# The second layer's front on the spectrum by image pairs, with repeated rows in one transfer

## The chip, the cores and the metric

The kernel runs on one core of one Trainium2 chip. The core has TensorE (PE in the profile, its weight loads PEld), VectorE (DVE), ScalarE (ACT), GpSimd (POOL) and SyncE (SP, which issues most transfers; ACT issues some too), 16 DMA engines, SBUF as working memory and PSUM[...]. The metric is device time in microseconds (us) of one execution; the median over the runs counts, and lower is better.

## The reference

The input x is four images of 48x48 positions and 128 channels. Two layers are applied, each as x + layer(gn(x)), where gn normalises over groups of four channels. Layer 0 is a selective scan: an input projection, a 3x3 depthwise convolution, and for each of four scan directions a linear recurrence over 2304 positions with 16 states for 256 channels, then a normalisation, a gate and an output projection. Layer 1 reads the same array differently. It takes each image as 48 "time" planes of 48x128 pixels and does a spectral attention over them:

```
xa   = x.reshape(B * T, 1, H, W)                # 192 planes of 48 x 128
xa_n = inorm(xa)                                # per plane: mean 0, variance 1
k, q = fno(xa_n, wK), fno(xa_n, wQ)             # 32 heads, at half the resolution
v    = fno(xa_n, wV)                            # 32 heads, at full resolution
attn = softmax(q k^T / sqrt(d))                 # 48 x 48 for each image and head
att  = inorm(fno(attn v, wP) + xa)
m    = fno(fno(inorm(att), wM0), wM1)           # two more spectral layers, gelu between
out  = inorm(m) + att
```

fno is a spectral convolution (a 2-D Fourier transform, a complex weight on the low frequencies, the inverse transform) plus a pointwise product. All data are float32.

## The kernel before

`layer0` (from L54) works image by image and, for each, through four directions of five chunks of 480 positions (the last of them 384). A chunk has 16 steps, one per state. A step is spread over the engines: ACT computes the decay (`da`), DVE multiplies `db` (three steps in four; POOL the fourth) and runs the scan `h`, POOL multiplies `hc`, and PE sums `yp`. SP fetches the rows `cbc` and `bbc` for a step five steps before they are read out. `advance` writes this order out by hand: `on` keeps the order of the program on each engine. After every step `advance` calls `piece`, which runs one piece of a generator in the list `later`: the projections of the next direction, the `front` of the next image (group statistics, projection in, convolution), or `back`, which finishes a chunk and stores it to `x1_dram`. While the last image (image 3) is worked on there is no next front, so `later` holds projections and backs only. The buffer rings of layer 0 nearly fill SBUF.

`layer1` uses `nc` for most of its first half. Such instructions are put into each engine's order by a planner, which goes by the program's order, its own costs and what each instruction depends on; it may draw them forward into idle time of layer 0's end. The front of layer 1 does, in this order of the program: load constants and `xa` (L745, all four images, 192 planes at once); `gw`, the products of wP and wV, transposed and stored as `dgt` with each row written 16 times (L779 to L794); `spectral_weights` (L950), which makes the 96x96 matrices of the last two spectral layers and stores them as `sp_d`; group statistics by `gblk` copies and bn_stats (L993, L994), and the affine pass over `xa` (L1000); `first_norm` (L695), with mean and variance of each plane by products with `mean_m` (L700, L711); `prepare`, which loads wQ and wK in small pieces (L894 to L900) and multiplies them to `g_qk`; `forward_w` (L724), the transform along W by products with `fw` (L730), scaled by the plane's 1/deviation and written to DRAM; `load_a2`, which reads it back with h on the partitions (L741); transposes of `xa` into `pair_t` (L1024); and the selection of frequencies for q and k and the plain part (L1042 to L1073).

Then come the scores (L1109 to L1138, with `keys` beside them storing `dxt`), the softmax, and the readout (L1196 to L1274). The readout goes over two image pairs and four groups of eight frequencies. A group has three tiles `xrep` of 16 time rows each, with every row on eight partitions: two images by eight copies of 16 rows, 16 transfers of 72 KB a tile from SP (L1228). It has four tiles `grep` (L1236). For each tile and each of the four `grep`, DVE and POOL multiply to `v` and `v3`, and PE sums `acc` (L1253). `xrep`, `v` and `v3` have two buffers, `grep` four. The weights `wpv` and `mask` are loaded just ahead (L1196, L1197). The last part, from `p0` on, is two strands of 96 planes through the inverse transforms and the two spectral layers.

Of the kernel before, what the change touches and what calls it, by code (L numbers as in the profile page):

```python
# [53 lines left out]
def layer0(ctx, tc, io, x1_dram):  # L54
# [8 lines left out]
    const = ctx.enter_context(tc.tile_pool(name="l0_const", bufs=1))  # L63
    one = ctx.enter_context(tc.tile_pool(name="l0_one", bufs=1))
# [4 lines left out]
    small = ctx.enter_context(tc.tile_pool(name="l0_small", bufs=2))  # L69
    ps_s = ctx.enter_context(tc.tile_pool(name="l0_pss", bufs=1, space=PSUM))  # L70
    ps_b = ctx.enter_context(tc.tile_pool(name="l0_psb", bufs=1, space=PSUM))
    ps_a = ctx.enter_context(tc.tile_pool(name="l0_psa", bufs=1, space=PSUM))
# [185 lines left out]
    def front(b, made):  # L258
# [20 lines left out]
        yield  # L279

# [306 lines left out]
    for j, chunks in enumerate(directions):  # L587
# [9 lines left out]
        for m, c in enumerate(chunks):  # L597
            c.carry = carries[j % 2]
            for i in range(N):
                if k == ORDER[0] and b + 1 < B and m > 1 and coming is None and not any(g in later for g in backs):  # L600
                    coming = front(b + 1, images[b + 1])
                    later.append(coming)
                if i in (N // 2 + 3, N // 2 + 6):
                    f = int(i > N // 2 + 3)
                    if m + 1 < len(chunks):
                        while not (j or chunks[m + 1].ready):
                            piece()
                        drive(chunks[m + 1], f)
                    elif nxt is not None:
                        drain(nxt)  # L610
                        drive(directions[j + 1][0], f)
                advance(Step(c, i))
                if not chunks[-1].ready and not j:
                    piece()
    for _ in range(len(window)):
        advance(None)
    while later:
        piece()

# [24 lines left out]
def layer1(ctx, tc, io, x1_dram, out):  # L644
# [5 lines left out]
    nc = tc.nc  # L650
    img = ctx.enter_context(tc.tile_pool(name="l1_img", bufs=1))
    const = ctx.enter_context(tc.tile_pool(name="l1_const", bufs=1))
    small = ctx.enter_context(tc.tile_pool(name="l1_small", bufs=2))
    dram = ctx.enter_context(tc.tile_pool(name="l1_dram", bufs=1, space=DRAM))
# [9 lines left out]

    ident = load("ident1", [128, 128], io["c_ident"])
    gmat = load("gmat1", [128, 128], io["c_group"])
    fw = load("fw", [128, 66], io["c_FW"])
    fh = load("fh", [96, 96], io["c_FH"])
    fhi = load("fhi", [96, 96], io["c_FHI"])
    ih = load("ih", [96, 96], io["c_IH"])  # L670
    eps = const.tile([128, 1], F32, name="eps1")
    nc.gpsimd.memset(eps, 1e-5)
    mean_m = const.tile([128, 128], F32, name="mean_m")
    nc.gpsimd.memset(mean_m, 1.0 / (H * W))
    n_g = everywhere("n_g", io["L1_norm_g"], 6)
# [3 lines left out]

    turn = [0]  # L680

    def either():
        turn[0] += 1
        return nc.gpsimd if turn[0] % 3 == 0 else nc.vector
# [8 lines left out]
    def per_image(t, n=HB):  # L693
        return t[:, None, :].to_broadcast([128, n, BT])

    def first_norm(psum, work, x):

        pm = psum.tile([128, 512], F32, tag="st", name="pm_in")
        for q in range(H // 2):
            nc.tensor.matmul(pm[:, 0 : 2 * BT], mean_m, x[:, 2 * q : 2 * q + 2], start=(q == 0), stop=(q == H // 2 - 1))  # L700
        m = small.tile([128, BT], F32, tag="in_m", name="in_m")
        nc.scalar.copy(m, pm[:, 0:BT])
        nc.vector.tensor_add(m, m, pm[:, BT : 2 * BT])
        pv = psum.tile([128, 512], F32, tag="st", name="pv_in")
        for q in range(0, H, HB):
            d = x[:, q : q + HB]
            either().tensor_sub(d, d, per_image(m))
            sq = work.tile([128, HB, BT], F32, tag="blk", name=f"sq_{q}")
            nc.scalar.activation(sq, d, AF.Square)
            for j in range(0, HB, 2):  # L710
                nc.tensor.matmul(  # L711
                    pv[:, 0 : 2 * BT], mean_m, sq[:, j : j + 2], start=(q + j == 0), stop=(q + j == H - 2)
                )
        r = small.tile([128, BT], F32, tag="in_r", name="in_r")
        nc.scalar.copy(r, pv[:, 0:BT])
        nc.vector.tensor_add(r, r, pv[:, BT : 2 * BT])
        nc.scalar.activation(r, r, AF.Sqrt, bias=eps)
        nc.vector.reciprocal(r, r)
        nc.vector.tensor_scalar(r, r, n_g[:, 0:1], None, ALU.mult)
        return r  # L720

    def forward_w(psum, work, src, r, name):


        da = dram.tile([2, 33, H, BT], F32, name=f"da_{name}")
        for q in range(0, H, HB):
            a = work.tile([66, HB, BT], F32, tag="blk", name=f"a_{name}{q}")
            for j in range(0, HB, 2):
                p = psum.tile([128, 512], F32, tag="mm", name=f"pa_{name}{q}_{j}")
                nc.tensor.matmul(p[0:66, 0 : 2 * BT], fw, src[:, q + j : q + j + 2], start=True, stop=True)  # L730
                nc.vector.tensor_mul(
                    a[:, j : j + 2], p[0:66, 0 : 2 * BT].rearrange("p (a t) -> p a t", t=BT), per_image(r, 2)[0:66]
                )
            nc.sync.dma_start(da.rearrange("c k h t -> (c k) h t")[:, q : q + HB], a)
        return da

    def load_a2(a2, da, n):
        for c in range(2):
            for i, s in enumerate(range(0, n, 11)):
                e = min(s + 11, n)  # L740
                dmas[i % 2].dma_start(a2[c * 48 : (c + 1) * 48, s:e], da[c, s:e].rearrange("k h t -> h k t"))  # L741

    xa = img.tile([128, H, BT], F32, name="xa")
    for b in range(B):
        dmas[b % 2].dma_start(xa[:, :, b * T : (b + 1) * T], x1_dram[b])  # L745

    pair_t = [img.tile([128, H, 128], F32, tag=f"p{p}", name=f"xnt{p}") for p in range(2)]
    sp_d = [dram.tile([96, 32, 96], F32, name=f"sp_d{i}") for i in range(2)]
# [4 lines left out]
    dgt = dram.tile([4, NH, 16, 3 * NC], F32, name="dgt")  # L753
    with ExitStack() as pw:
        ps_t = pw.enter_context(tc.tile_pool(name="l1_wt", bufs=2, space=PSUM))
        q1 = pw.enter_context(tc.tile_pool(name="l1_w1", bufs=1))

        w_p = q1.tile([128, 12, 2, NH], F32, name="w_p")
        w_v = q1.tile([128, 6, 2, NH], F32, name="w_v")
        d48 = [q1.tile([128, 128], F32, name=f"d48{c}") for c in range(2)]  # L760
        for c in range(2):
            dmas[c].dma_start(w_p[:, :, c], io["wP"][c].rearrange("(j p) h -> p j h", p=128))
            dmas[c].dma_start(w_v[:, :, c], io["wV"][c].rearrange("(j p) h -> p j h", p=128))
            dmas[c].dma_start(d48[c], io[("c_D48r", "c_D48i")[c]])
        for c in range(2):
            p = ps_t.tile([128, 512], F32, tag="tr", name=f"pv48{c}")
            nc.tensor.matmul(p[:, 0:NH], d48[c], w_v[:, 0, c], start=True, stop=True)
            nc.scalar.copy(w_v[:, 0, c], p[:, 0:NH])
        gw = q1.tile([128, 12, 3, NH], F32, name="gw")
        for c in range(2):  # L770
            nc.vector.tensor_mul(gw[:, :, c], w_p[:, :, c], ws_v[:, None, :].to_broadcast([128, 12, NH]))
        half = [128, 6, NH]
        for c in range(2):
            g6 = gw[:, 0:6, c]
            t1 = q1.tile(half, F32, tag="gt", name=f"gt{c}_0")
            nc.vector.tensor_mul(t1, w_v[:, :, c], ws_p[:, None, :].to_broadcast(half))
            nc.vector.tensor_add(g6, g6, t1)
            for i in range(2):

                t2 = q1.tile(half, F32, tag="gt", name=f"gt{c}_{i + 1}")  # L780
                nc.vector.tensor_mul(t2, w_p[:, 0:6, i], w_v[:, :, (c + i) % 2])
                (nc.vector.tensor_sub if c == 0 and i == 1 else nc.vector.tensor_add)(g6, g6, t2)
        nc.vector.tensor_add(gw[:, :, 2], gw[:, :, 0], gw[:, :, 1])

        for k in range(4):
            gt = q1.tile([NH, 3, NC], F32, name=f"gtt{k}")
            for c in range(3):
                p = ps_t.tile([128, 512], F32, tag="tr", name=f"pgt{k}_{c}")
                for j in range(3):
                    nc.tensor.transpose(p[0:NH, j * 128 : (j + 1) * 128], gw[:, 3 * k + j, c], ident)  # L790
                nc.scalar.copy(gt[:, c], p[0:NH, 0:NC])
            nc.sync.dma_start(
                dgt[k], gt.rearrange("h c n -> h (c n)")[:, None].to_broadcast([NH, 16, 3 * NC])
            )  # L794
# [29 lines left out]
    def prepare():  # L824
# [30 lines left out]

        cqk = pe.tile([T, NH], F32, name="cqk")
        nc.vector.tensor_mul(cqk, ws_q[0:T], ws_k[0:T])
        nc.vector.tensor_mul(
            d_qk, ident[0:T, None, 0:T].to_broadcast([T, NH, T]), cqk[:, :, None].to_broadcast([T, NH, T])
        )  # L860
        with ExitStack() as pw:
# [21 lines left out]
            def weights(side, name, ws, gen, zero, mirror):  # L883
# [949 lines left out]
```

## Time and profile before

| what | us |
|---|---|
| median of 3 runs | 5072.27 (5071.78 to 5079.84) |
| the profiled execution | 5081.34 |
| its span, first to last instruction | 5079.4 |
| layer 0, to the issue of the last x1 store | to 4200.6 |
| front of layer 1, to the first product f of the scores | 4200.6 to 4407.4 |
| scores and softmax | 4407.4 to 4515.5 |
| wpv, mask and a0 | 4515.5 to 4543.8 |
| readout | 4543.8 to 4812.6 |
| inverse transforms, spectral layers, output | from 4814.3 |
| busy in the whole span | PE 4207.3, DVE 4169.1, POOL 4034.6, ACT 2923.0 |
| mean granted TensorE clock | 0.929 |

The chain of waits follows the work that ended last back from the end, at each step to what released it; what stands in it sets the time. Busy time by stretch tells whether an engine fills a stretch. A wait names the engine and line that waited, what ended the wait, the total in us, how often, and the longest.

### The profile page before, as it was taken

Reading aid. Unit: us, or ns where it says so; the run is one execution under the profiler, and the core shown is the slowest. Engines: PE = TensorE matmul, PEld = TensorE weight load, DVE = VectorE, ACT = ScalarE, POOL = GpSimd, SP = SyncE. Lnnn points to the kernel's source line nnn. Section 1 sums busy time; section 2 is a strip of 40 time slices with the busy share of each in tenths; the row PEclk is TensorE's granted clock in tenths of the full one; section 3 lists DMA queues with packets and bytes.
Section 4 is the critical chain, followed back from the end, with each engine's and each line's share of the span. In section 5 each row is a group of like instructions: output and inputs, shape, how many; then the busy total and the mean of one; then the engine's idle time right before and its main releaser. Section 6 shows DMA issues by size and latency. Waiting matters only on the chain. (4 is left out here: it accounts for less than half of the span.)

```text
span 5079.4 us, 44364 instructions
## 1 busy us (share of the span) xinstructions
PE 4207.3 (83%) x12344; PEld 1893.5 (37%) x12344; DVE 4169.1 (82%) x2888; ACT 2923.0 (58%) x6467; POOL 4034.6 (79%) x2219
## 2 busy tenths in 40 slices
PE   6889898888798988887989888878787785888876
PEld 2334333333343333333433333333333332453343
DVE  3689998989899989898999898999999873356636
ACT  3566566666565666665656666656666652223334
POOL 4589998988899989888999898999999873246532
PEclk9989999999899999998999999999999987889977
DMA  1223232322233323222333232333332216236646
GB/s 54 73 88 101 92 114 92 101 88 98 94 106 105 106 91 101 88 98 94 106 103 107 91 102 88 97 105 106 100 103 92 97 66 131 59 82 171 162 106 153
DMA packets 276766, 509.25 MB, mean 100 GB/s; under 512 B 100602, under 2 KB 185434, under 8 KB 276326
## 3 DMA queue, kind: packets, MB, share of 16 engines
q1 hardware_dynamic: 265318, 502.61, 32.5%
q10 hardware_dynamic: 11200, 3.81, 0.5%
q8 instruction: 97, 1.59, 0.1%
q14 instruction: 151, 1.24, 0.1%
HBM read 462.58 MB, written 43.72 MB: 100 GB/s over the span
## 5 line engine op out<-in xcount | busy, mean ns | idle before, releaser
L50 POOL TENSOR_TENSOR hc<-h,cbc 128x960 f32<-128x960 f32 (+1 forms) x1280 | 2719.7, 2140 | 449.2 <-DVE h L50 338.4
L50 DVE TENSOR_TENSOR_SCAN h<-da,carry,db 128x961 f32<-128x961 f32 (+1 forms) x1280 | 2702.4, 2129 | 153.8 <-ACT carry L50 106.0
L50 ACT ACTIVATE da<-dt,a_neg 128x480 f32<-128x480 f32 (+1 forms) x2560 | 1661.3, 649 | 1233.9 <-DVE h L50 1189.3
L50 PE MATMUL yp<-hc,ident 128*128 128x480 f32 (+1 forms) x5120 | 2273.9, 572 | 6.6 <-POOL hc L50 6.4
L50 PEld LDWEIGHTS yp<-hc,ident 128*128 128x128 f32 x5120 | 1006.3, 198 | 1409.7 <-issue 1018.9
L50 DVE TENSOR_TENSOR db<-du,pb 128x960 f32<-128x960 f32 (+1 forms) x960 | 1063.8, 1108 | 232.2 <-PE pb L50 176.8
L50 POOL TENSOR_TENSOR db<-du,bbc 128x960 f32<-128x960 f32 (+1 forms) x320 | 688.6, 2152 | 0.0
L50 PE MATMUL pb<-bs,pick 112*128 112x480 bf16 (+1 forms) x960 | 359.2, 374 | 391.3 <-DVE db L50 389.9
L50 PE MATMUL pc<-pad,cdiag 128*128 128x480 f32 (+1 forms) x630 | 284.6, 564 | 9.0 <-ACT pad L50 9.0
L1249 POOL TENSOR_TENSOR v<-grep,xrep 128x768 f32<-128x768 f32 x96 | 174.1, 1820 | 115.9 <-PE acc L1253 57.7
L1253 PE MATMUL acc<-v,attn_c 128*64 128x384 f32 x1152 | 214.8, 514 | 28.0 <-POOL v L1249 17.8
L1245 DVE TENSOR_TENSOR v<-gp,xrep 128x1536 f32<-128x1536 f32 x96 | 165.1, 1754 | 86.8 <-DMA xrep<-dxt 35.2
L50 POOL TENSOR_TENSOR du<-dt,xc 128x480 f32<-128x480 f32 (+1 forms) x160 | 205.0, 1282 | 37.2 <-ACT dt L50 37.2
L50 ACT COPY db<-carry 128x1 f32<-128x1 f32 x1280 | 226.7, 177 | 7.5 <-DVE db L50 4.2
L50 PE MATMUL px<-xc,w_xp 128*112 128x480 f32 (+1 forms) x320 | 215.0, 759 | 17.0 <-ACT xc L50 13.3
L50 PEld LDWEIGHTS <-pick 112*128 112x128 bf16 x960 | 97.9, 102 | 335.4 <-issue 311.8
L50 ACT ACT_TABLE_LOAD x147 | 188.6, 1283 | 25.7 <-PE gv_g L50 13.8
L50 PE MATMUL pd<-xd,w_dt 8*128 8x480 f32 (+1 forms) x320 | 167.6, 604 | 39.3 <-ACT bs L50 24.4
L50 ACT COPY carry<-h 128x2 f32<-128x2 f32 x1024 | 193.2, 189 | 0.0
L50 PEld LDWEIGHTS pc<-pad,cdiag 128*128 128x128 f32 x630 | 122.1, 195 | 142.4 <-issue 114.7
L50 PE MATMUL yp<-y,ident 128*128 128x480 f32 (+1 forms) x240 | 164.6, 815 | 0.2
L1253 PEld LDWEIGHTS acc<-v,attn_c 128*64 128x64 f32 x1152 | 89.8, 142 | 149.2 <-issue 65.8
(366 smaller groups left out, 3128.9 us busy)
## 6 DMA issues: line engine op xcount, KB each, us to landing
cbc<-cd SPq DMA_DIRECT2D x512, 480.0 KB
bbc<-cd SPq DMA_DIRECT2D x256, 240.0 KB
cbc<-cd SPq DMA_DIRECT2D x128, 384.0 KB
xrep<-dxt SPq DMA_DIRECT2D x384, 72.0 KB
grep<-dgt SPq DMA_DIRECT2D x32, 576.0 KB
bbc<-cd SPq DMA_DIRECT2D x64, 192.0 KB
dgt<-gtt SPq DMA_DIRECT2D x4, 2304.0 KB
x<-in_xT SPq DMA_DIRECT2D x16, 288.0 KB
```

Of the source, the lines that this page charges most:

```text
L50: return lambda *args, **kw: self._tc.keep_in_program_order(emit(*args, **kw))
L1245: nc.vector.tensor_mul(v, gp[:, None, :, 0:NC].to_broadcast([128, 2, 2, NC]), x[:, :, 0:2])
L1249: nc.gpsimd.tensor_mul(v3, r[:, 2:3].to_broadcast([128, 2, NC]), x[:, :, 2])
L1253: nc.tensor.matmul(acc[c][64 * b : 64 * b + 64, 0:NC], attn_c[:, 2 * pair + b, g, q], v[:, b, c] if c < 2 else v3[:, b], start=first, stop ...
```

## The change

Layer 1's program now opens by running layer 0 inside itself (`first_layer`), so that its own tiles can be laid on the right-hand side of SBUF.

- The input images go to `x_in`, two tiles of an image pair each, on the right-hand side. Images 0 to 2 are loaded whole, image 3 by the chunks in which layer 0 stores it.
- The front is done by pairs p = 0 and 1. `statistics` runs bn_stats straight on `x_in`. The affine pass is dropped: its scale goes into the transform's weights (`fwa`), its shift into a bias (`fwb`). The plane's mean is taken off the lowest frequency of the transform, averaged over h (`over_h`), and its 1/deviation `r` is multiplied onto `a2` after the reload instead of before the store. `first_norm` gets means and variances by products with 32 columns to four partition quarters, and writes x - mean to `xa`. Pair 0 is left to the planner (`by = nc`), pair 1 is in program order (`by = on`).
- `spectral_weights` becomes `matrices`, a generator in `later` of layer 0 while image 3 is worked on. The same generator arranges wQ and wK in DRAM (`d_w`, `d_m`); `products` (the second half of `prepare`) loads them with two transfers a side.
- `gw` comes after the pairs in the program, and `dgt` holds each row once.
- `xrep` is loaded by two transfers a tile with a leading repeat of 8, `grep` with each row repeated 16 times in the transfer, `wpv` and `mask` by 8 and 3 transfers.
- `ih` is loaded ahead of the last part. Pools change their order (`ps_a` first in PSUM, `small` earlier).

```diff
+    def matrices():
+        room = one.tile([128, 9, 128], F32, tag="cdiag", name="matrices")
...
+        general = [(0, 0, 8), (8, 12, 12), (20, 8, 4)]
+        for of, name in enumerate(("wQ", "wK")):
+            at_8 = 24 + 4 * of
+            for c in range(2):
...
+                for o, r, m in general + [(at_8, 8, 4)]:
+                    for j in range(4):
+                        k = int(j == 0)
+                        nc.sync.dma_start(dst[j][k:, o : o + m], src[j][k:, r : r + m])
+                    yield FREE
...
+        for n in range(2):
+            for k in range(0, 32, 2):
+                for c in range(2):
+                    for i in range(2):
+                        on.scalar.activation(m[3 + 2 * c + i], m[2], AF.Copy, scale=w[:, n, c, k + i : k + i + 1])
+                    if c == 0:
+                        yield FREE
+                p = side(f"psp{n}_{k}")
+                for c in range(2):
+                    on.tensor.matmul(
+                        p[0:96, 0:192],
+                        m[c],
+                        room[:, (3 + 2 * c) * 96 : (5 + 2 * c) * 96],
+                        start=(c == 0),
+                        stop=(c == 1),
+                    )
+                yield
+                on.scalar.copy(room[:, 7 * 96 : 9 * 96], p[0:96, 0:192])
+                nc.sync.dma_start(
+                    sp_dram[n][:, k : k + 2].rearrange("p k m -> p (k m)"), room[:, 7 * 96 : 9 * 96]
+                )
+                yield FREE
...
+                if k == ORDER[0] and b + 1 == B and m > 1 and coming is None and not any(g in later for g in backs):
+                    coming = matrices()
+                    later.append(coming)
...
+    x_in = [imgs.tile([128, 2, H, T], F32, tag=f"p{p}", name=f"x_in{p}") for p in range(2)]
+    for b in range(B):
+        for s, n in CHUNKS if b == B - 1 else [(0, L)]:
+            h = slice(s // T, (s + n) // T)
+            nc.sync.dma_start(x_in[b // 2][:, b % 2, h], x1_dram[b][:, h])
...
+    def forward_w(psum, work, p, x, aff):
...
+        for b in range(2):
+            by.vector.tensor_scalar(fwa[:, b], fw, aff[:, 0, b : b + 1], None, ALU.mult)
...
         for q in range(0, H, HB):
+            a = work.tile([66, HB, 2, T], F32, tag="a", name=f"a_{p}_{q}")
+            for b in range(2):
+                pa = psum.tile([128, 512], F32, tag="mm", name=f"pa_{p}_{q}_{b}")
+                by.tensor.matmul(pa[0:66, 0 : HB * T], fwa[:, b], x[:, b, q : q + HB], start=True, stop=True)
...
+            nc.scalar.dma_start(
+                da.rearrange("c k h t -> (c k) h t")[:, q : q + HB], a.rearrange("p h b t -> p h (b t)")
+            )
+            yield
...
+    def first_norm(psum, work, p, x, aff, y):
...
+        for q in range(0, 24, HB):
+            for i, b, h in quarters:
+                by.tensor.matmul(
+                    pm[32 * i : 32 * i + 32, 0 : HB * T],
+                    a_m[:, b : b + 1].to_broadcast([128, 32]),
+                    x[:, b, h + q : h + q + HB],
+                    start=(q == 0),
+                    stop=(q == 16),
                 )
...
+        for i, b, h in quarters:
+            d = y[:, h : h + 24, p * 96 + b * T : p * 96 + (b + 1) * T]
+            by.vector.scalar_tensor_tensor(
...
+            by.scalar.activation(sq, d, AF.Square)
+            yield
+            for q in range(0, 24, HB):
+                by.tensor.matmul(
+                    pv[32 * i : 32 * i + 32, 0 : HB * T], mean_m, sq[:, q : q + HB], start=(q == 0), stop=(q == 16)
                 )
...
+        for p in range(2):
+            aff = statistics(psst, p, x_in[p])
+            norm = first_norm(psst, work, p, x_in[p], aff, xa)
+            trans = forward_w(psum, work, p, x_in[p], aff)
+            next(norm)
+            next(trans)
+            next(norm)
+            for _ in range(5):
+                next(trans)
+                next(norm)
+            das.append(next(trans))
+            rs.append(next(norm))
...
+            on.tensor.matmul(p0[0:H, 0:96], over_h, a2p[0:H, 0], start=True, stop=True)
+            on.vector.tensor_sub(a2p[0:H, 0], a2p[0:H, 0], p0[0:H, 0:96])
+            for s, e in ((0, 17), (17, 33)):
+                v = a2p[:, s:e]
+                on.vector.tensor_mul(v, v, rs[p][0:96, None, :].to_broadcast([96, e - s, 96]))
+            on.vector.tensor_scalar(a2p[0:H, 0], a2p[0:H, 0], b48[0:H], None, ALU.add)
+        products()
...
                     for b in range(2):
-                        for i in range(8):
-                            nc.sync.dma_start(
-                                x[16 * i : 16 * i + 16, b].rearrange("p c n -> p (c n)"),
-                                dxt[2 * pair + b, k, q * 16 : q * 16 + 16],
-                            )
+                        nc.sync.dma_start(
+                            x[:, b].rearrange("p c n -> p (c n)"),
+                            dxt[2 * pair + b, k, q * 16 : q * 16 + 16][None].to_broadcast([8, 16, 3 * NC]),
+                        )
...
                                 r.rearrange("p c n -> p (c n)"),
-                                dgt[k, 8 * g : 8 * g + 8].rearrange("h r n -> (h r) n"),
+                                dgt[k, 8 * g : 8 * g + 8][:, None].to_broadcast([8, 16, 3 * NC]),
```

## The prediction

> **What bounds the kernel now.** I read the page first, then the chain of work that ended last from 4150 us on, the busy time by stretch, and last the waits of the readout stage. The page has DVE, POOL and PE all near 80% of 5079.4 us, but that is layer 0, which runs to 4200. The change works mostly after it, where no engine is full. The chain there, from the end of layer 0 to the first score product:
>
> ```profile
> 4208.69 22.03 DMA xa<-x
> ...
> 4258.87 18.07 PE pm_in L700 x48
> ...
> 4285.94 13.18 PE pv_in L711 x40
> ...
> 4318.17 6.69 PE psw L977 x10
> ...
> 4363.26 12.62 DMA a_x<-da_x
> ...
> 4387.58 9.46 PE psel L1042 x158
> ...
> 4407.37 3.43 DVE f L1120 x2
> ```
>
> Columns are start, length, work. The front is a queue of whole-batch steps: load, statistics, mean, variance, spectral weights of the last blocks, W transform, reload, selection. From 4200.6, when the last x1 store is issued, to 4407.4 it takes 206.8 us. By stretch (span, then busy us and instructions of PE, weight loads, DVE, ACT, POOL; clock; DMA share; GB/s):
>
> ```profile
> 4200.00:4225.00 25.00, 1.83 (x7) 1.21 (x7) 10.38 (x29) 4.71 (x12) 11.72 (x61) 0.54 0.95 203
> ...
> 4250.00:4275.00 25.00, 16.52 (x45) 9.67 (x46) 6.53 (x10) 1.55 (x2) 0.03 (x1) 0.80 0.99 201
> ```
>
> No engine fills a stretch: a latency chain, so what is moved off it is gained whole. The readout (4544 to 4811) is different. SP's own timeline and two of its waits:
>
> ```profile
> 4534.55 33.54 SPq L1228 DMA_DIRECT2D xrep<-dxt  x48
> 4568.20 1.78 SPq L1236 DMA_DIRECT2D grep<-dgt  x4
> 4570.07 30.44 SPq L1228 DMA_DIRECT2D xrep<-dxt  x48
> ```
>
> ```profile
> DVE v L1245 <- DMA xrep<-dxt: 35.2, 13, 3.5
> ...
> POOL v L1249 <- DMA xrep<-dxt: 20.7, 11, 3.0
> ```
>
> SP issues without a break, 48 row copies in 30 us per group of eight frequencies, and DVE and POOL wait for their landing. PE idles 2.1 us in each of the eight groups just before the third tile; the other 3.6 us of its idle time per group (1.42 + 0.57 + about 1.6) lie at the group's edge and come from the zt chain.
>
> [...] The trace agrees on the count: between 4182.6 and 4191 us it holds 117 four-byte landing packets for 17 small copies with 1 to 12 rows, where 16 each would be 272. The trace of before has no large copy with a leading repeat. [...] The trace: the quickest quarter of the 4608-byte packets took 0.18 us or less, 25.6 GB/s. [...] The trace agrees:
>
> ```profile
> 4849.48 0.85 PE L50 MATMUL st_y<-sqy,one_m 128*32 128x384 f32 x8
> ```
>
> Eight passes to four column tiles in 0.85 us, where one takes 0.49.
>
> **The change part by part.**
>
> *Image load.* 22.0 us of xa<-x leave the chain for images 0 to 2, if their buffers are free. By my sum layer 0's pools take about 205 KB per partition, so the new right-hand tiles lie over its last pool, the ring of dt and bs. Those are last read near 4162 to 4171; 3.5 MB at 200 GB/s is 18 us, so they land before 4190. What stays is the last chunk: store issued 4200.6, landed about 4203, load landed about 4205. The repeated 9.4 MB of dgt stores (0.99 DMA share at 4250) shrink to 0.6 MB.
>
> *Statistics.* The 24 gblk copies (0.51 us) and the affine pass (5.7 us) go. Image pair 0 runs under layer 0's tail (4171 to 4200, PE and DVE mostly idle). For pair 1 two bn_stats (2 x 0.55), the aggregate 0.3 and the group chain (4249.1 to 4253.2: 4.0, table load included): affine known at 4211.
>
> *Pair 1 on PE.* Mean: 12 products of 128x384 on four column tiles; by the line above 24 passes are 2.6 us. W transform: 12 x 2 x 0.486 = 11.7. Variance: each quarter's three products sit in one column tile with two 66-column products between quarters, so I count no overlap: 4 x 2.9 = 11.7, three quarters of it ahead of the last transform. With 2.2 for weights and row sums: 2.6 + 2.2 + 11.7 + 8.7 = 25.2, last transform at 4236. DVE (two-input passes of 128x1152, about 1.3 us by L1120's 1.75 for 1536) and ACT (1.1 us squares, 0.47 us copies) have less per round.
>
> *Reload.* Store about 2.7 us, then 1.25 MB in rows of 384 B, half of before's 768: 12.6 us took 2.4 MB, so between 6.3 (by bytes) and 12.6 (by rows); I take 8. Landed at 4247. New after it: the row-mean product, subtraction and two multiplications of 96x1632 (1.8 each by the same row), 5 us: 4252. Behind these DVE instructions are products() (about 45 small ones and the 1.74 us d_qk, 12 us), and for them waits g_qk, needed 23 us later: hidden under selection.
>
> *What PE must still fit in.* The transposes pxn (15.6) and wP/wV transposes (8.8) go into the gap of pair 1's reload (4239 to 4252) and before 4211, where pair 0's variance (11.7) also wants to be. Some 6 to 8 us do not fit: selection starts at 4259, not 4252. Selection to f is unchanged (4383.2 to 4407.4 = 24.2): f at 4283 to 4291; I take 4287. **Front: -120.** Bounds: -140 (all fits, reload 6.3), -90 (planned work put ahead of pair 1, or the load late).
>
> *Spectral weights and wQ/wK under image 3.* Out of the front: 30 us of spw/psw, part of the 120. Added to layer 0: 64 products of 96x192 (2 x 0.25 each: 32 us PE), 128 ACT scalings of 96x96 (0.24: 31 us), 32 copies (0.32: 10 us), some 136 small copies on SP's queue (0.3 to 0.4 us to issue: 48 us), in about 130 pieces of one per step. Queued behind them on SP are cbc and bbc, issued five steps (16 us) before their use; on ACT the decay, which has two buffers. Cover: the 3.0 us of DVE per step. Like for like: a whole front with more PE work makes image 2's directions 260, 240 and 245 us against image 3's 249, 237 and 240. I take **+4**, bounds 0 and +20 (the front's whole cost); without cover, PE and ACT in turn, 73.
>
> *Mask and wpv.* Between 4515.5 and 4526.9 SP issues 16 loads at 0.42 in the chain; now 6: 2.5 + 2.2 landing. **-6** (0 to -7).
>
> *Readout.* Issue per tile falls from 16 to 2. But xrep and grep both have a leading repeat of 8[...]: 8 x 24.5 GB/s = 196 (24 per engine is what a 386 GB/s burst of 16 shows). A group needs 6 + 4 copies, 5.9 MB: 30.1 us. PE needs 27.7 busy + 3.6 = 31.3, so the wait at the third tile (2.1 x 8 = 17 us) can go only if the burst at the group's edge (four grep, then xrep) fits 1.2 us of slack. I take a third of it: **-6**; bounds -20 (16 engines), +15 (22 GB/s per engine: 33.5 plus edge).
>
> *ih.* No longer kept: its load follows fw64, issued 4812.7, landing near 4816; pe_p starts at 4814.3 now. **+2** (0 to +3).
>
> Sum: -120 + 4 - 6 - 6 + 2 = -126. The profiled execution took 5081.3 (span 5079.4 and 1.9 around it), 9.0 over the median of 5072.3; I take the difference off the median: **4946**.
>
> **The rivals.**
> *Eight engines bind the readout.* [...] Against: packets at 25.6 GB/s. At 20 GB/s per engine a group takes 37 us, 8 x 3.5 = 28 more than now: 4946 + 6 + 28 = 4980.
> *Front gains less.* The loads wait for all of layer 0, or work placed by the planner stands before pair 1's chain. Then 18 us of load and the 14 of pair 0's PE work return: 4978; with PE alone setting the end some 4990.
> *All fits.* Front -140, readout -20: 4912.
> *Slower.* One place: the pieces in image 3. Each must cost DVE 1.0 us for 130 pieces to eat 130 us; at 1.1 the kernel takes 5072 + 16 = about 5088. The carry copies among Exp cause no table loads (2 in a whole direction), SP's lead is 16 us, so I hold it unlikely.
>
> **How the numbers follow.** As summed (own range 4925 to 4966): 0.52. Readout bound: 0.17. Front less: 0.15. All fits: 0.12. Slower: 0.03; no change 0.01. The range 4906 to 4990 takes in all but the outer parts of the rivals. 0.2%, about 10 us, is what a measurement of this kernel can tell from no change (its three runs lie 8 us apart). Faster 0.96, same 0.01, slower 0.03.
>
> **What would show it.** Right: x_in loads landing before 4195, the first f some 87 us after the last x1 store is issued (206.8 before); group period 32 to 33 us in the readout with SP mostly idle; eight landing packets per xrep; image 3's directions within 5 us. Wrong: DVE or POOL waiting longer for xrep or grep than now; a DMA share near half in the readout with waits (eight of 16 engines full); PE idle in pair 1's transform; image 3's first direction back near 260 us or over.

## The result and the profile after

The changed kernel takes 5117.84 us (median of 4 runs, 5113.96 to 5127.24) against 5072.02 for the kernel before (4 runs, 5065.55 to 5079.84, on the same chip): a ratio of 1.0092, interval 1.0073 to 1.0112. It is slower by some 46 us, where 4946 was forecast. The profiled execution took 5127.24 us with a span of 5125.1, 45.7 more than the 5079.4 of before.

Split at the events that the forecast uses, the two spans differ as follows. All figures are from the two traces, in us.

| stretch | before | after | difference | forecast |
|---|---|---|---|---|
| start to the issue of the last x1 store (layer 0) | 4200.6 | 4221.1 | +20.5 | +4 |
| to the first f (front) | 206.8 | 98.0 | -108.8 | -120 |
| to the last score product | 108.1 | 107.8 | -0.3 | 0 |
| to the first acc product (mask, wpv, a0, first loads) | 28.4 | 36.4 | +8.0 | -6 |
| first to last acc product (readout) | 265.5 | 393.0 | +127.5 | -6 |
| to the end | 270.0 | 268.7 | -1.3 | +2 |
| sum | 5079.4 | 5125.1 | +45.7 (differences rounded) | -126 |

So the part of the change that was meant to be large worked, and the readout, which had been booked at -6, cost more than that part gained. First the front, in the chain of work that ended last (start, length, work):

```profile
4188.88 11.19 ACTq L1087
...
4225.82 3.93 PE pm L866 x24
...
4252.32 2.07 PE pm L50 x24
...
4302.21 6.63 PE psel L1170 x158
...
4319.17 3.43 DVE f L1248 x2
```

The 22 us of image load and the 31 us of whole-batch mean and variance of before are gone. What is left is two pairs in turn: the first pair's mean starts only at 4225.82, after the last store, the second's at 4252.32. The first line is ACT's queue standing in the issue of the w_v load; it comes back below.

The next piece of the same chain, from the last score product to the readout:

```profile
4427.01 7.90 DMA wpv<-in_wVs
...
4435.57 6.08 DMA wpv<-in_wPs
...
4447.04 14.32 DMA xrep<-dxt
...
4473.41 11.88 DMA xrep<-dxt
```

Two loads of wpv, 128 words each, are waited for one after the other, and then one xrep tile takes 14.32 us to land. The busy time by stretch (span, then busy us and instructions of PE, weight loads, DVE, ACT, POOL; clock; DMA share; GB/s), a piece of the front and one of the readout:

```profile
4225.00:4250.00 25.00, 23.39 (x97) 8.65 (x97) 13.98 (x31) 9.05 (x15) 4.86 (x30) 0.91 0.17 52
...
4550.00:4600.00 50.00, 32.77 (x148) 13.56 (x150) 22.39 (x15) 10.82 (x15) 21.78 (x12) 0.76 0.49 112
```

In the front PE is now nearly full, 23.4 of 25 us. In the readout no engine is, and the transfers stand at 0.49 of their 16 engines at 112 GB/s: eight engines busy all the time, at 14 GB/s each. Over the readout of before (4560 to 4800) the same view has:

```profile
4560.00:4800.00 240.00, 198.58 (x1074) 84.57 (x1072) 156.89 (x106) 76.41 (x106) 153.02 (x85) 0.95 0.64 173
```

SP's own timeline there, against 48 row copies in 30 us of before, and what the engines wait for between 4560 and 4800 us (total, times, longest):

```profile
4591.42 8.26 SPq L1365 DMA_DIRECT2D grep<-dgt  x4
4599.78 37.86 SPq L1357 DMA_DIRECT2D xrep<-dxt  x6
```

```profile
ACT gp L1372 <- DMA grep<-dgt: 98.1, 18, 11.4
...
DVE v L1374 <- DMA xrep<-dxt: 34.0, 10, 6.0
```

SP has ten transfers to issue per group of eight frequencies instead of 52, and spends the time waiting for buffers to come free. The wait named first is not among those of before: ACT's copy of grep to gp waits up to 11.4 us for its load.

### The profile page after: what moved, and what is told of

It is laid out like the page before. It is cut to its first block, busy times and chain, and to the rows that moved or that the text cites. A ratio compares the mean times of both kernels' runs of the same rounds, so it can differ in the third digit from the quotient of the medians.

```text
span 5125.1 us, 44257 instructions
## 1 busy us (share of the span) xinstructions
PE 4223.3 (82%) x12444; PEld 1903.4 (37%) x12444; DVE 4163.8 (81%) x2901; ACT 2952.7 (58%) x6608; POOL 3996.0 (78%) x2188
## 4 chain that ended last, share of the span: by engine, by line
DVE 17%; PE 14%; issue 7%; ACT 7%; DMA 6%; POOL 2%; SPq 1%; ACTq 0%; DVEq 0%; POOLq 0%
DVE h L50 12%; PE yp L50 4%; ACT da L50 3%; DMA grep<-dgt 3%; DVE db L50 3%; DMA xrep<-dxt 2%; PE acc L1382 1%; ACT L50 1%; PE sc L1255 1%; PE pi_p L50 1%; POOL db L50 1%; ACT dt L50 1%; POOL v L1378 1%; DVE m L50 1%; POOL hc L50 1%
## 5 line engine op out<-in xcount | busy, mean ns | idle before, releaser
L1382 PE MATMUL acc<-v,attn_c 128*64 128x384 f32 x1152 | 253.1, 575 | 112.0 <-ACT s L1390 67.6
L1372 ACT COPY gp<-grep 128x768 f32<-128x768 f32 x96 | 77.1, 803 | 297.9 <-DMA grep<-dgt 158.7
```

The costliest lines, as they stand in the source:

```text
L1372: nc.scalar.copy(gp[:, :, 0:NC], r[:, 0:2])
L1382: nc.tensor.matmul(acc[c][64 * b : 64 * b + 64, 0:NC], attn_c[:, 2 * pair + b, g, q], v[:, b, c] if c < 2 else v3[:, b], start=first, stop ...
```

## Experiments

**The transfer forms by themselves.** The kernel holds nothing but loads of 4608-byte rows from DRAM to SBUF. Each form fills 128 partitions (two of them fewer) and is issued four times in a row. The kernel was run once, and so was the next one.

```
r16, r8 = x[0:16], x[0:8]                      # rows of 1152 words
t[:, i] <- r16[None].to_broadcast([8, 16, N])   # as xrep: 8 copies, 16 rows
t[:, i] <- r8[:, None].to_broadcast([8, 16, N]) # as grep: 8 rows, 16 copies
t[:, i] <- r16[:, None].to_broadcast([16, 8, N])
t[:, i] <- x.rearrange("(r h) n -> h r n", h=8) # 8 x 16, all rows different
t[:, i] <- x                                    # 128 rows
...
```

> Both layers are left out and the output is zeros; only transfers of 4608-byte rows run, each form four times in a row and alone on the chip. Three theories for the halved rate per engine (13.3 GB/s in the changed kernel's readout, about 25 in the kernel before). Same rows (engines that read one row together hinder each other): the repeat of 16 rows eight times in the order copy, row is slow (about 110 GB/s in all); eight rows repeated 16 times with the row outermost, each engine with its own row, about 200; the 128 different rows split as 8 by 16 about 200; 16 by 8 with the row outermost over 300; 16 by 8 with the repeat outermost slow. Few engines (eight engines have only half of their rate, whatever they read and wherever they write): every form with 8 outermost about 110, every form with 16 outermost over 300, 4 outermost about 55, and eight engines writing only 32 partitions also about 110. Destination (an engine that writes 16 partitions in a row collides with the next ones): every 8 by 16 form about 110, 16 by 8 forms between 110 and 380, and eight engines writing 4 partitions each (32 in all) about 200. The 16-row copies of the kernel before: 250 to 386, by the issue of 0.3 us each.

Measured (engines: landing packets per transfer, which the shares of 0.25, 0.5 and 0.9 in the view below bear out; packet: median time of a 4608-byte packet; rate over the stretch):

| form, outermost first | engines | packet, ns | GB/s |
|---|---|---|---|
| 8 copies of 16 rows (xrep) | 8 | 326 | 120 |
| 8 rows, 16 copies each (grep) | 8 | 311 | 123 |
| 8 by 16, all rows different | 8 | 318 | 125 |
| 16 rows, 8 copies each | 16 | 300 | 220 |
| 16 copies of 8 rows | 16 | 319 | 227 |
| 16 by 8, all rows different | 16 | 311 | 227 |
| 128 rows in a row | 16 | 178 | 322 |
| 4 copies of 32 rows | 4 | 178 | 96 |
| 8 copies of 4 rows, 32 partitions | 8 | 178 | 141 |
| 16 copies of 4 rows, 64 partitions | 16 | 361 | 201 |
| 16-row copies as before | 16 | 400 | 150 |

The busy time by stretch of this kernel, with only DVE and POOL ahead of clock, DMA share and GB/s, for four of the rows (xrep's form, 16 rows of 8 copies, 128 rows, 4 copies of 32):

```profile
20.42:40.14 19.72, 0.00 (x0) 0.00 (x0) 1.00 0.51 120
...
64.56:75.27 10.71, 0.00 (x0) 0.00 (x0) 1.00 0.90 220
...
123.60:130.95 7.35, 0.00 (x0) 0.00 (x0) 1.00 0.89 322
133.61:158.14 24.53, 0.00 (x0) 0.00 (x0) 1.00 0.25 96
```

Two theories fall. Different rows are as slow as repeated ones (125 against 120 and 123), so it is not the reading of one row by many engines. And eight engines reach 178 ns when they write 4 partitions each, so eight engines are not slow as such; sixteen take 300 to 319 ns in all three 16 by 8 forms. The destination is left: which partitions are written at the same time. Two of the expected numbers missed: eight engines with 4 partitions each reached 141 GB/s where about 200 was expected, and the 16-row copies of before reached 150 where 250 to 386 was. SP's issue, one copy of 74 KB every 0.46 us, allows them 160. Their packets take 400 ns; the 128-row load has 178 ns, 25.9 GB/s while an engine writes.

**The destination moved.** The next kernel keeps the access pattern, the eight engines and the bytes, and moves only where the 64 partitions lie:

```
t[0:64, i]   <- x[0:8][None].to_broadcast([8, 8, N])
t[32:96, i]  <- x[0:8][None].to_broadcast([8, 8, N])
t[64:128, i] <- x[0:8][None].to_broadcast([8, 8, N])
```

> Both layers are left out and the output is zeros; only transfers of 4608-byte rows run, each form eight times in a row. [...] the plain 128-row transfer 178 ns per packet and some 320 GB/s; 16 groups of 8 different rows, groups not mergeable, about 300 ns and 225; eight engines with 8 partitions each on partitions 0 to 63 about 310 ns and 110 to 130, the same on 64 to 127, but on partitions 32 to 95, [...]178 ns and 170 to 200; 16 engines with 2 partitions each on 0 to 31 about 350 ns and 200; eight with 4 each on 0 to 31 178 ns. Rival (the number of engines or the shape of the access pattern alone): 0 to 63 and 32 to 95 equal.

Its first numbers are those of the destination theory. Why 32 to 95 should be the quick partitions was not shown by any trace: it was my assumption.

The same view; the stretches are partitions 0 to 63, 32 to 95, 0 to 63 again, 64 to 127:

```profile
50.52:69.17 18.65, 0.17 (x1) 0.00 (x0) 1.00 0.50 127
71.98:85.11 13.13, 0.17 (x1) 0.00 (x0) 1.00 0.50 180
87.35:107.19 19.84, 0.17 (x1) 0.00 (x0) 1.00 0.51 119
109.97:127.93 17.96, 0.17 (x1) 0.00 (x0) 1.00 0.50 131
```

Same engines, same bytes, same share of 0.50: 119 to 131 GB/s on partitions 0 to 63 and 64 to 127, 180 on 32 to 95. The packets take 304 to 345 ns on 0 to 63, 262 on 64 to 127 and 178 on 32 to 95. So the rival falls, and in this comparison the destination theory holds. The 128-row load ran at 353 GB/s here (178 ns), sixteen groups of eight different rows at 230 GB/s. One number missed: 16 engines with two partitions each had packets of 193 ns, not 350. At 200 GB/s that form was near the limit of SP's issue (147 KB every 0.65 us), so it decides nothing. Nor is a long run of partitions per engine slow as such: if each engine takes one of the outermost indices, as the four and the eight landing packets suggest, an engine writes 32 partitions in the form of 4 copies of 32 rows, and its packets took 178 ns, against 311 to 326 with 16 partitions in the 8 by 16 forms. What is shown is that the destination decides; by which mechanism stays open.

**The transfers in the kernel: alone, and undone.** One kernel is the kernel before with the new xrep, grep and dgt; the other is the changed kernel with these three as before.

```diff
-                        for i in range(8):
-                            nc.sync.dma_start(x[16 * i : 16 * i + 16, b]..., dxt[2 * pair + b, k, q * 16 : q * 16 + 16])
+                        nc.sync.dma_start(x[:, b]..., dxt[2 * pair + b, k, q * 16 : q * 16 + 16][None].to_broadcast([8, 16, 3 * NC]))
...
-                                dgt[k, 8 * g : 8 * g + 8].rearrange("h r n -> (h r) n"),
+                                dgt[k, 8 * g : 8 * g + 8][:, None].to_broadcast([8, 16, 3 * NC]),
```

> The kernel before with this part of the change alone: one transfer with eight repeats for each half of an xrep tile, dgt stored once and grep repeated 16 times in the reading; front, layer 0, mask and wpv as before. My theory: the readout takes 390 to 400 us in place of 269, less some us for the smaller dgt stores: total 5072 + 120 to 130 = about 5197 (5185 to 5205). Rival (the slow readout needs the new front too): below 5100.

> The changed kernel with its readout's transfers undone: eight copies of 16 rows for each xrep tile, dgt stored 16 times over and grep read as 128 rows in a row. My theory (the readout's eight engines at half rate cost 127.5 us there, and nothing else in the readout is lost): the readout returns to about 269 us, total 5118 - 127 + 0 to 8 for the larger dgt stores = about 4993 (4980 to 5005). Rival (the readout is slow for another reason, a buffer that lies elsewhere or the front's work that runs into it): it stays above 350 us and the total above 5070.

Alone: 5185.16 us, ratio to before 1.0231 (1.0213 to 1.0248). The readout takes 390.2 us against 265.5, and its waits are those of the changed kernel, without its front:

```profile
ACT gp L1240 <- DMA grep<-dgt: 112.6, 19, 12.7
```

Undone: 5019.11 us, ratio 0.9905 (0.989 to 0.9919); the readout takes 258.6. So the transfers account for the 127.5 us. My sum for the undone kernel was 26 us too low, and the front shows why: 132.5 us from the last store to the first f, against 98.0 with dgt stored once. The 9.4 MB of repeated dgt stores run through the front and cost 34.5 us there: the transfers are at a share of 0.97 to 0.99 from 4250 to 4300, and the reload of a_x stands 26.95 us in the chain. In the kernel before, storing once gained 24.7 (206.8 to 182.1). This gain lay within the front's -120 and had no price of its own. The repeated reading thus bought 25 to 35 us in the front for 125 in the readout.

**The other order of the partitions.** With row, head in place of head, row, both repeats have 16 outermost. The order is that of attn_c's partitions as well, so the softmax writes its transposed rows in this order, and mask and wpv follow.

```diff
-                sn = p2.tile([128, 3, 8, 16], F32, tag="sn", name=f"sn{t}")
+                sn = p2.tile([128, 3, 16, 8], F32, tag="sn", name=f"sn{t}")
...
-                            dxt[2 * pair + b, k, q * 16 : q * 16 + 16][None].to_broadcast([8, 16, 3 * NC]),
+                            dxt[2 * pair + b, k, q * 16 : q * 16 + 16][:, None].to_broadcast([16, 8, 3 * NC]),
...
-                                dgt[k, 8 * g : 8 * g + 8][:, None].to_broadcast([8, 16, 3 * NC]),
+                                dgt[k, 8 * g : 8 * g + 8][None].to_broadcast([16, 8, 3 * NC]),
```

> The changed kernel with the partitions of the readout in the order row, head in place of head, row: both repeats then have 16 outermost (xrep 16 rows each repeated 8 times, grep 8 rows repeated 16 times), two transfers per tile as in the changed kernel. Few engines: all 16 at about 24 GB/s, readout 255 to 272 us, total about 4980 (4965 to 4995). Same rows: xrep fast, grep slow (all 16 engines read one row at a time): readout 300 to 340 us, total 5020 to 5060. Destination: each engine writes 8 partitions in a row, half of the gain: readout about 300 us, total about 5020.

5002.75 us, ratio 0.9871 (0.9857 to 0.9886): the sign of the change turns by the order of two dimensions. The readout takes 261.4 us. The stretch and the same wait:

```profile
4550.00:4600.00 50.00, 39.87 (x199) 20.21 (x195) 29.64 (x22) 15.09 (x21) 28.36 (x16) 0.86 0.83 194
```

```profile
ACT gp L1372 <- DMA grep<-dgt: 43.1, 16, 7.3
```

That is 1.7 times the rate, 194 GB/s (16 x 8 ran at 220 to 230 alone), and grep is still waited for, up to 7.3 us. PE is busy again. The 261.4 us hit the number that I had set beside "few engines", a theory which the forms by themselves refute, so that hit is luck; beside the destination I had set about 300. At 194 GB/s the 5.9 MB of a group take 30 us, less than the 32.7 us that a group lasts here, so the slower packets of this form (300 to 319 ns alone, against 178 for 128 rows) cost far less than half of the gain. The total is 23 us above the 4980 of "few engines". By the traces the span is 124.6 us shorter than the changed kernel's: readout -131.6, the first loads -4.2, the front +3.7, the end +6.2. The last two, and the 9.4 us by which the changed kernel's profiled execution lies over its median, make up most of the 23.

**Layer 0: the copies and ACT's loads.** Image 3's four directions (from first scan to first scan; the last to its last scan) take 249.4, 237.4, 239.5 and 264.3 us before, 262.1, 240.7, 238.3 and 263.0 after. The 12.7 us lie in the last chunk of the first direction. SP's timeline there:

```profile
3376.08 5.39 SPq L306 DMA_DIRECT2D d_w<-in_wQ  x8
3382.43 0.37 SPq L503 DMA_DIRECT2D cbc<-cd  x1
...
3411.07 4.30 SPq L312 DMA_DIRECT2D d_m<-in_wK  x7
3415.41 0.58 SPq L507 DMA_DIRECT2D bbc<-cd  x1
```

A copy of weights takes 0.49 to 0.78 us of SP (median 0.59); 81 of them, with the gaps between them, take 52.6 us between 3376 and 3442, and the scan's loads stand between. One kernel leaves these copies out (136; the expectation says 132 by a miscount):

```diff
-        for of, name in enumerate(("wQ", "wK")):
-            ...
-                        nc.sync.dma_start(dst[j][k:, o : o + m], src[j][k:, r : r + m])
-            ...
-                        nc.sync.dma_start(d_m[of][o + i : o + i + 1, c], io[name][c][r - i : r - i + 1])
```

> The changed kernel without the 132 small copies of wQ and wK into DRAM under image 3 (left out; the scores' weights are then wrong), the spectral weights as they are. My theory (SP's queue, full of copies of 0.6 to 0.75 us each, makes the scan's loads late): image 3's first direction falls from 262 to 249 to 251 us, the other directions stay within 2 us, total about 5106. Rival (the PE, ACT or buffer work of the new pieces costs it): it stays above 258 us.

The first direction falls to 250.7 us, the last store to 4207.8 from 4221.1; one time of 5110.34 us. The spectral pieces, which moved into the same stretch, do not slow it. So the copies are the cause. The waits of that stretch name them in the changed kernel:

```profile
POOL db L50 <- DMA d_w<-in_wK: 8.5, 2, 5.7
POOL db L50 <- DMA d_m<-in_wK: 8.2, 1, 8.2
```

POOL's db does not read the copies but the bbc row: the one that SP issued at 3415.41, behind seven copies, is that of the db which starts at 3420.74 after the wait of 8.2. A wait for several transfers is put down to one of them.

The rest of the 20.5 us is the tail, from the last scan to the last store: 33.9 us before, 40.8 after. The other kernel makes ACT's three loads wait for the second pair's affine values:

```diff
+                if c:
+                    for t in (w_p[:, 0, 1, 0:1], w_v[:, 0, 1, 0:1], d48[1][:, 0:1]):
+                        nc.vector.tensor_copy(t, aff[:, 0, 0:1])
                 dmas[c].dma_start(w_p[:, :, c], ...)
```

> The changed kernel, with ACT's loads of w_p, w_v and d48 made to wait for the second pair's affine values, so that they no longer stand in ACT's queue ahead of the last image's norm. My theory (ACT is held 11.2 us in the issue of w_v while the image loads fill the transfers, and the last x1 store waits for ACT): the last store comes some 8 to 11 us earlier, total 5118 - 10 = about 5108 (5104 to 5112). Rival (the norm then waits for something else in the same stretch, the loads' own bandwidth or POOL): less than 3 us.

The mechanism was right in the main, the total wrong. The tail falls to 33.6 us, so these loads on ACT's queue did cost 7. But the total is 5126.78 us, ratio to before 1.011 (1.0093 to 1.0127), no better than the changed kernel: the front grew from 98.0 to 111.5 us. In this trace the late loads move the transposes of dgt (pgt) from 4224 to 4263 down to 4257 to 4279, into the second pair's work on PE, where there is no gap.

**Put together.** Three kernels with the row, head order and fewer copies. A layout of the copies' buffer with j ahead of the partitions lets three of four general copies go in one (104 in place of 136), and at most three go per piece:

```diff
-                    for j in range(4):
-                        k = int(j == 0)
-                        nc.sync.dma_start(dst[j][k:, o : o + m], src[j][k:, r : r + m])
+                    nc.sync.dma_start(dst[0][1:, o : o + m], src[0][1:, r : r + m])
+                    nc.sync.dma_start(dst[1:, :, o : o + m], src[1:, :, r : r + m])
```

They differ in the loads of w_p, w_v and d48: late as above, all on SP, or as in the changed kernel.

> The changed kernel with three repairs: the readout's partitions in the order row, head (16 outermost), ACT's late loads as above, and the small copies fewer (104 in place of 136, by a layout of their buffer in which three of four come in one) and at most two or three per step. By the runs so far: 5003 for the order, less 8 to 11 for ACT, less 4 to 12 for the first direction of image 3: about 4984 (4975 to 4995).

> The readout in the order row, head and the fewer copies as in a_best2, but all loads of w_p, w_v and d48 on SP's queue, behind the image loads, with no wait added. My theory (in a_best2 the late loads pushed the dgt transposes under the selection, 11 us, while freeing ACT gained 7): both are had, front near 100 us from the last store, total 4988 - 8 = about 4980 (4972 to 4988). Rival (the loads on SP now hold the last x1 store, which is queued behind them): 4990 or more.

> The readout in the order row, head and the fewer copies, with the loads of w_p, w_v and d48 where the changed kernel has them. My theory: 5003 less the 11 to 13 us of image 3's first direction = about 4990 (4984 to 4996), and ACT's wait of some 11 us in the issue of w_v is still there. Rival (the fewer copies only move the wait to a later direction): 4998 or more.

| | us | ratio to before | last store | front | readout |
|---|---|---|---|---|---|
| late loads | 4988.44 | 0.9836 (0.9822 to 0.9851) | 4195.8 | 108.9 | 267.6 |
| on SP | 4973.73 | 0.9808 (0.9793 to 0.9822) | 4197.6 | 98.2 | 264.7 |
| as changed | 4973.14 | 0.9808 (0.9792 to 0.9823) | 4196.5 | 98.1 | 267.6 |

The first direction of image 3 is back at 249.4 us in all three. The last was expected at 4990 and came 17 us lower. Against the row, head kernel its second direction is 5.0 us shorter as well, its last one 7.5 and its front 3.6, and ACT's stand is 5 us where it was 11:

```profile
4170.28 5.07 ACTq L1088
```

So placing the loads on SP, which I had thought worth 8 us, gains nothing over leaving them. The tail from the last scan to the last store is 39.5 to 39.6 us in all three, wherever these loads stand: the 7 us of the late loads in the changed kernel do not come again here, and what sets the tail instead was not looked for. Both kernels of 4973 us beat the kernel before by some 96 us, where the changed one loses 46. The readout is not faster in them than before (265.5), although SP issues ten transfers a group in place of 52: the fewer issues themselves gained nothing there.

## Why the prediction was wrong

**Image load, statistics, pairs on PE: the front.** Forecast -120 (-140 to -90), measured -108.8. The mechanism is right; two terms were too good. "they land before 4190" was off. SP issues the first image only at 4185.80, and the transfers are far from full in part of the time that follows:

```profile
4185.80 19.73 SPq L769 DMA_DIRECT2D x_in<-x  x7
...
4190.00:4195.00 5.00, 0.71 (x2) 0.00 (x0) 2.60 (x6) 0.00 (x0) 0.00 (x0) 1.00 0.31 115
4195.00:4200.00 5.00, 0.00 (x0) 0.00 (x0) 0.27 (x1) 0.00 (x0) 0.00 (x0) 0.54 0.90 367
```

SP stands 10.4 us between these issues in a wait that the profile puts down to ACT's load of w_p, and issues the four chunks of image 3 that are ready only at 4203.8 to 4205.1. In the kernel with the late loads they go out from 4192.2 to 4199.7. So ACT's early loads of the weights held up the image loads too. And "Image pair 0 runs under layer 0's tail" did not happen. DVE's timeline:

```profile
4192.40 2.86 DVE L806 BATCH_NORM_STATS2 st<-x_in 128x6 f32<-128x384 f32 x6 [3.64 <-DMA x_in<-x]
4203.90 0.56 DVE L1095 TENSOR_TENSOR gw<-w_p,ws_v 128x384 f32<-128x384 f32 x1 [8.63 <-DMA x_in<-x]
```

DVE has one image's statistics done by 4195 and then stands 8.63 us ahead of gw, which reads w_p, with the rest of pair 0 queued behind it. Pair 0's affine values are there at 4225.2, not before 4200, and its 25 us of PE come after the last store. That is the mechanism of the rival "front gains less", at a third of its price (11 of 32 us). The mean on four column tiles took 3.93 us for 24 passes in the first pair and 2.07 in the second (2.6 by the sum; 11.7 if they did not overlap), so the overlap of column tiles that the prediction read from the `st_y` line held. One reading was wrong without harm to the sum: "No engine fills a stretch: a latency chain" passes over the transfers, at a share of 0.95 and 0.99 in the lines beside it. The smaller dgt stores are part of what the front gained.

**Spectral weights and wQ/wK under image 3.** Forecast +4, bounds 0 to +20; measured +20.5. The failed step is "0.3 to 0.4 us to issue" together with the "five steps (16 us)" of lead: the copies from DRAM to DRAM cost SP 0.65 us each with the gap to the next, come up to eight in a row, and ate the lead. It cost 12.7 us, and image 3's first direction at 262.1 us is one of the signs that the prediction had named for being wrong. The 32 us of PE and 41 of ACT for the spectral weights, on which the sum spent its words, cost little that shows (the two middle directions are +3.3 and -1.2). The 7 us of the tail were in no step: ACT issues w_p and w_v ahead of the last image's norm and stands 11.19 us in the issue of w_v while the image loads are under way. Why an issue stands so long is open, since the transfers were at a share of 0.31 for five of these 11 us. The sum asked what stands on SP behind the copies, and not what stands on ACT behind its loads.

**Mask and wpv.** Forecast -6, measured +8.0. The two-by-two of the runs splits it: with only the new mask and wpv the stretch takes 32.4 us, with only the new xrep and grep 32.9, with both 36.4, with neither 28.4. Each costs 4: the word loads of wpv queue one behind another and land late, and the first xrep lands late. The sum had 0.42 us for an issue and 2.2 for the landing; the issues took 0.59 to 0.74 and the last word load landed after 6.08.

**Readout.** The step that failed and decided the sign is "8 x 24.5 GB/s = 196". The count was right (592 landing packets for 74 transfers of xrep and grep, eight each), the rate per engine was 14 to 15. At 116 GB/s the 5.9 MB of a group take 51 us; the readout's 393.0 us are 49.1 per group, where 30.1 was the sum. The rate had been taken from a burst in the kernel before, where grep came in 128-row loads (178 ns a packet when alone), and carried over to a form with eight engines, whose packets take 311 to 326 ns alone. "22 GB/s per engine" as the lower bound rested on nothing that limited it from below: the trace of before has no large load of this form. Alone it ran at 120 to 123 GB/s, 15 per engine, and that is near what the readout got.

**The rivals.** "Eight engines bind the readout" named the place, and its sign in the profile (a share near half, with waits) is what came. But its price stopped at 20 GB/s per engine. With the forecast's other gains of 120 us, the readout turns the sign at about 33.2 + 15 = 48 us per group, which is 5.9 MB / 48 us / 8 = 15.4 GB/s per engine: the rival should have been carried on to there, and was the true mechanism of "slower". The rival that was given for "slower", pieces at 1.0 us each in image 3, was not what happened.

**ih.** Forecast +2, measured 1.5 (PE stands 3.29 us ahead of pe_p against 1.75): right.

## What to carry to other kernels

The rate of a transfer belongs to its form (96 to 353 GB/s here for 4608-byte rows into 128 partitions): before a new form replaces one that the trace shows, count the engines that it gets, look at which partitions it writes, and if the trace has no such form, time it by itself. A repeat with 16 outermost ran at 220 to 227 GB/s here and one with 8 outermost at 120 to 123, and the order of the partitions was free to choose. A step moved under other work is moved past every queue that its instructions and transfers stand in: count what is issued in a row, at the price of that kind of copy (0.65 us with the gap here, up to eight in a row), and see what is behind it.

## What the runs showed of the hardware that was not expected

- Eight engines with the same pattern and bytes ran at 119 to 127 GB/s on partitions 0 to 63, at 131 on 64 to 127 and at 180 on 32 to 95.
- A 4608-byte packet took 178 ns in the load of 128 rows, in 4 copies of 32 rows, in 8 copies of 4 rows and in 8 copies of 8 rows on partitions 32 to 95. It took 262 to 361 ns in the 8 by 16 and 16 by 8 forms, in 16 copies of 4 rows, and in 8 copies of 8 rows on 0 to 63 or 64 to 127. So four engines in 4 copies of 32 rows ran at 96 GB/s, only a fifth below the 120 of eight engines in the 8 by 16 form.
- A small copy from DRAM to DRAM held SP's queue for 0.49 to 0.78 us (median 0.59, 3376 to 3442 us); the same weights' loads into SBUF held it for 0.22 to 0.30 in the kernel before (4180 to 4190 us).
- A load's issue itself stood 11.19 us on ACT's queue while three images (3.5 MB) were being loaded, and everything behind it on that engine stood too; the transfers were at a share of 0.31 for part of that time.
